# Quantising a convolution's weights beside an involution: where its steps stand in a row, and where the extremes of the first weights are taken

## The chip, the core and the metric

The kernel runs on one core of a Trainium2 chip. The core has TensorE (PE: matrix products, with weight loads shown apart as PEld), VectorE (DVE), ScalarE (ACT), GpSimd (POOL) and SyncE (SP, which here only issues transfers). The engines run side by side and wait for each other through semaphores; each takes its instructions in the order of its own queue. The time is the device time of one execution in microseconds (us), and a kernel's time is the median of its runs.

## The reference

The input is `x`, 8 images of 256 channels and 56 x 56 pixels in float32. Two layers follow each other, each adding its result to its input.

```python
def _L0_conv_ref(x, w_reduce, b_reduce, w_span, b_span):      # an involution, K = 7, G = 16
    ker = einsum('bchw,oc->bohw', x, w_reduce) + b_reduce
    ker = einsum('bchw,oc->bohw', ker, w_span) + b_span       # 49 taps for each pixel and group
    ...
    return (ker * patches).sum(axis=3)                        # over the 7 x 7 neighbourhood

def ternary_quantize(x):
    mx, mn = (jnp.max(x), jnp.min(x))
    lo, hi = mn + (mx - mn) / 3, mx - (mx - mn) / 3
    return jnp.where(x < lo, -1.0, jnp.where(x > hi, 1.0, 0.0))

def noised_tri_conv(x, w):                                    # 3 x 3, 256 to 256 channels
    tq = ternary_quantize(w - jnp.mean(w))
    return conv(x, tq) + einsum('bchw,oc->bohw', x, tq[:, :, 1, 1])

x = x + _L0_conv_ref(_gn(x), ...)                             # _gn: group norm of 32 groups
out1 = relu(batch_norm_train(noised_tri_conv(_gn(x), w1), g1, b1))
out2 = batch_norm_train(noised_tri_conv(out1, w2), g2, b2)
x = x + relu(out1 + out2)
```

The weights `w1` and `w2` (256 x 256 x 3 x 3 each) must therefore be reduced to three numbers each (mean, lower and upper threshold) before any of their elements can be quantised.

## The kernel before

The work has three parts in time. The first is the involution, from the start to about 1170 us. The second is the two convolutions, and the third a last pass over all images that adds `x`, `out1` and `out2`.

**The involution** goes over the 8 images in 4 quarters of 64 channels each, 32 quarters, and over each quarter in 10 rows (`ty`), 320 rows. A row stands for three lines of the image's halves. In a row:

- `apply_row` (PE, L808) multiplies the quarter's matrices `a` with the row's pixels `q` into the PSUM tile `pa`; `transpose_q` (PE L742, ACT L745) makes part of the `q` of later rows, the rest is loaded by `prefetch` (SP, L735) four rows ahead.
- `pick_out` takes `pa` to `inv` (ACT L820, once per row; DVE L821) and adds it to `x` (POOL L824).
- `generate` makes the next quarter's matrices, 14 units per quarter, of which `PER_ROW` gives each row 2, 1 or, in the last row, 0: PE L775 into one of two PSUM tiles `pg`, from which ACT (L779) and DVE (L784) write `a`. A unit's `pg` can be filled again only when they have read the unit two before.
- in between stand the next image's normalisation: statistics (DVE L149), padded strips (`prep`: POOL L667, PE L710, ACT L713, stores from SP at L701), and in an image's third quarter `reduce` (PE L644, ACT L649).

**The order** of each engine's queue is that of the text: `pin()` at a row's end ties each instruction behind the one before it on its engine. Deferred stores stand in the list `tasks`; `transfer(2)` issues up to two of them at the head of a row.

**The weights** are quantised inside these rows by the generator `quantize`, first for `w1`, then for `w2`; from row 8 (`QUANT_AT`) each row runs it to its next `yield`, after `pick_out` and ahead of the row's units of `generate` (L963). For each of the two it takes:

- the extremes, six times: a load of 384 KB (L210), then in the next row a maximum and a minimum (DVE L212, L213) and a sum (ACT L214, in place, hence behind them), then a row with nothing; after the sixth, small operations over five rows make mean and thresholds, with three small PE products (L227, L228, L235). 23 rows.
- 16 pieces of 6 rows: a load of 144 KB (L260); three operations of 288 columns (L263 to L265); two or three of 96 (L275, L279, L280); four of 96 (L282 to L285), after which the store of the seven slots (L288) is put in `tasks`; two rows with nothing. Of the seven stored slots six are used: `SLOT` names them for `weights`.

All pieces share one buffer. The quantised weights are read back from DRAM when the convolutions begin (L301).

**In front of the rows**, the first image is loaded (L545), zeros are stored round the scratch images (L630), the norm's parameters are made, and `reduce(0, py)` for three `py` and the 14 units of quarter 0 run together with the first strips. The tile `a1` that quarter 1's matrices will fill is idle there.

Of the kernel before, what the change touches and what calls it, by code (L numbers as in the profile page):

```python
# [8 lines left out]
F32 = mybir.dt.float32  # L9
F32R = mybir.dt.float32r  # L10
AF = mybir.ActivationFunctionType
ALU = mybir.AluOpType
AX = mybir.AxisListType
# [4 lines left out]
P = 128  # L18
B, C, H, W = 8, 256, 56, 56
HW = H * W  # L20
CT = C // P
# [9 lines left out]
GQ = G // NCQ  # L31
# [4 lines left out]
PY, PX = 3, 8  # L36
TY, TX = 10, W // PX
NP = PY * PX
NT = 2 * (TY - 1) * TX
NE = 2 * TX  # L40
# [15 lines left out]

UNITS = ((0, 3, 0), (3, 3, 0), (6, 2, 0), (8, 4, 2), (12, 4, 1), (16, 4, 2), (20, 4, 1))
NU = GP * len(UNITS)

PER_ROW = (2, 1, 2, 1, 2, 1, 2, 1, 2, 0)  # L60
NQB = 4
# [7 lines left out]
WT = 6  # L69
# [9 lines left out]


QN, QJ = 96, 3 * C // 96
QS = 3 + WT - 2
SLOT = (0, 3, 4, 5, 6, 2)
QM = 6


# [1 line left out]
def involution_tri_block_kernel(  # L88
# [3 lines left out]
    nc = tc.nc  # L92
# [11 lines left out]
    wq_d = [dram.tile([P, QS * CT * 3 * C], F32, tag=f"wqd{i}", name=f"wqd{i}") for i in range(2)]  # L104
# [83 lines left out]
        nc.vector.tensor_tensor(bi, beta, bi, ALU.subtract)  # L188
        return sc, bi

    def quantize(dst, w_dram, pool, transposer, psum_tile, tasks, name):


        nf = CT * 9 * C

        def piece():
            return pool.tile([P, (3 + QS) * QN], F32, tag="piece", name=f"piece_{name}")

        cols = pool.tile([P, 32], F32, tag="cols", name=f"cols_{name}")
        n_cols = [0]  # L200

        def col(n=1):
            n_cols[0] += n
            return cols[:, n_cols[0] - n:n_cols[0]]

        s, mx, mn = col(QM), col(QM), col(QM)
        f = nf // QM
        for j in range(QM):
            v = piece()
            nc.sync.dma_start(v[:, :f], w_dram[:, j * f:(j + 1) * f])  # L210
            yield
            nc.vector.tensor_reduce(mx[:, j:j + 1], v[:, :f], AX.X, ALU.max)  # L212
            nc.vector.tensor_reduce(mn[:, j:j + 1], v[:, :f], AX.X, ALU.min)  # L213
            nc.scalar.activation(v[:, :f], v[:, :f], AF.Identity, accum_out=s[:, j:j + 1])  # L214
            yield
            yield
        sums, ends = col(), col(2)
        nc.vector.tensor_reduce(sums, s, AX.X, ALU.add)
        nc.vector.tensor_reduce(ends[:, 0:1], mx, AX.X, ALU.max)
        nc.vector.tensor_reduce(ends[:, 1:2], mn, AX.X, ALU.min)  # L220
        nc.vector.tensor_scalar(ends[:, 1:2], ends[:, 1:2], -1.0, None, ALU.mult)
        v = piece()
        nc.vector.memset(v[:, :P], 1.0)
        yield

        ps = psum_tile(f"ends_{name}")
        nc.tensor.matmul(ps[:, P:P + 1], v[:, :P], sums, start=True, stop=True)  # L227
        nc.tensor.transpose(ps[:2, :P], ends, transposer)  # L228
        mean, top = col(), col()
        nc.vector.tensor_scalar(mean, ps[:, P:P + 1], 1.0 / (P * nf), None, ALU.mult)  # L230
        nc.vector.tensor_reduce(top[:2], ps[:2, :P], AX.X, ALU.max)
        nc.vector.tensor_copy(v[:2, P:2 * P], top[:2].to_broadcast([2, P]))
        yield
        ps = psum_tile(f"all_{name}")
        nc.tensor.transpose(ps[:, :2], v[:2, P:2 * P], transposer[:2, :2])  # L235
        ex = col(2)
        nc.vector.tensor_copy(ex, ps[:, :2])
        amx, amn = ex[:, 0:1], ex[:, 1:2]

        nc.vector.tensor_tensor(amx, amx, mean, ALU.subtract)  # L240
        nc.vector.tensor_scalar(amn, amn, -1.0, mean, ALU.mult, ALU.subtract)
        yield

        d, q0, r, th = (col() for _ in range(4))
        nc.vector.tensor_tensor(d, amx, amn, ALU.subtract)
        nc.vector.tensor_scalar(q0, d, 1.0 / 3.0, None, ALU.mult)
        nc.vector.scalar_tensor_tensor(r, q0, -2.0, d, ALU.mult, ALU.add)
        nc.vector.tensor_tensor(r, r, q0, ALU.subtract)
        yield
        nc.vector.scalar_tensor_tensor(th, r, 1.0 / 3.0, q0, ALU.mult, ALU.add)  # L250
        nc.vector.tensor_tensor(amn, amn, th, ALU.add)
        nc.vector.tensor_tensor(amx, amx, th, ALU.subtract)
        lo, hi = amn, amx
        yield
        for t in range(CT):
            for j in range(QJ):
                v = piece()
                w, u = v[:, :3 * QN], v[:, 3 * QN:]
                o = (t * QJ + j) * 3 * QN
                nc.sync.dma_start(w, w_dram[:, o:o + 3 * QN])  # L260
                yield
                g = u[:, :3 * QN]
                nc.vector.tensor_scalar(g, w, mean, hi, ALU.subtract, ALU.is_gt)  # L263
                nc.vector.tensor_scalar(w, w, mean, lo, ALU.subtract, ALU.is_lt)
                nc.vector.tensor_tensor(g, g, w, ALU.subtract)  # L265
                yield

                def part(x, k):
                    return x[:, k * QN:(k + 1) * QN]


                c0, c1 = max(C, j * QN) - j * QN, min(2 * C, (j + 1) * QN) - j * QN
                if c0 < c1:
                    g1 = part(u, 1)[:, c0:c1]
                    nc.vector.tensor_scalar(g1, g1, 2.0, None, ALU.mult)  # L275

                e, f = part(w, 0), part(w, 1)
                g0, g1, g2 = (part(u, k) for k in range(3))
                nc.vector.tensor_tensor(e, g0, g2, ALU.add)  # L279
                nc.vector.scalar_tensor_tensor(f, g2, 4.0, g0, ALU.mult, ALU.add)  # L280
                yield
                nc.vector.tensor_tensor(part(u, 3), e, g1, ALU.add)  # L282
                nc.vector.tensor_tensor(part(u, 4), e, g1, ALU.subtract)
                nc.vector.scalar_tensor_tensor(part(u, 5), g1, 2.0, f, ALU.mult, ALU.add)
                nc.vector.scalar_tensor_tensor(part(u, 6), g1, -2.0, f, ALU.mult, ALU.add)  # L285

                def store(u=u, o=t * 3 * C + j * QN):
                    nc.sync.dma_start(  # L288
                        bass.AP(dst[:].tensor, dst[:].offset + o,
                                [[QS * CT * 3 * C, P], [CT * 3 * C, QS], [1, QN]]), u)  # L290

                tasks.append(store)
                for _ in range(3):
                    yield

    def weights(i, k):

# [221 lines left out]
    with ExitStack() as ph1:  # L519
# [16 lines left out]
        fix = ph1.enter_context(tc.tile_pool(name="fix", bufs=1))  # L536
        xpool = ph1.enter_context(tc.tile_pool(name="xpool", bufs=2 * NCQ - 1, side="right"))
        work = ph1.enter_context(tc.tile_pool(name="work", bufs=2))

        def load_x(b, c, j):  # L540

# [68 lines left out]
        ident_sb = fixed([P, P], "ident_sb", ident)  # L610
# [16 lines left out]
        for d in (d for ds in xt_d for d in ds):  # L627
            for r0, n in ((0, PAD), (PAD + HH, HQ - PAD - HH)):
                e = n * QX * RP // P
                nc.sync.dma_start(  # L630
                    bass.AP(d[:].tensor, d[:].offset + r0 * QX * RP, [[e, P], [1, e]]), zero[:, :e])

        def reduce(b, py):

# [242 lines left out]
                gn1_stats(0, c, j)  # L877
        def matrices(m):
            return (apool if m % 2 == 0 else apool1).tile(
                [P, (NT * NP + NE * PX) * GQ], F32, tag=f"a{m % 2}", name=f"a_{m}")  # L880

        apool1 = ph1.enter_context(tc.tile_pool(name="apool1", bufs=1))
        qpool = ph1.enter_context(tc.tile_pool(name="qpool", bufs=NQB))
        pieces = ph1.enter_context(tc.tile_pool(name="pieces", bufs=1))
        pin(start=True)
# [1 line left out]
            pass  # L887
        strips, around = prep(0), surround(0, 0)
        a_next = matrices(0)

        for py in range(PY):
            next(strips)
            transfer(len(tasks))
            reduce(0, py)
        for u, _ in enumerate(generate(0, 0, a_next)):
            if u < 4 or u % 3 == 0 and u < 12:
                next(strips)
                transfer(len(tasks))
            elif u < 9:
                next(around)  # L900
            pin()
            if u == 5:
                for _ in range(NQB):
                    prefetch()
        for _ in around:
            pass


# [8 lines left out]
        for k in rows[:QLEAD]:  # L917
            transpose_q(*k)
        pin()
        norm = iter(())  # L920
        quant = chain(*(quantize(wq_d[i], v, pieces, ident_sb, ps_one, tasks, f"w{i + 1}")
                        for i, v in enumerate((w1, w2))))
        last = None
        for m, (b, c) in enumerate(quarters):
            a = a_next
# [6 lines left out]
            for ty in range(TY):  # L932
# [27 lines left out]
                    gn1_stats(b + 1, (r - 4) // NCB, (r - 4) % NCB)  # L960
                pick_out(b, c, ty, *row)
                next(norm, None)
                if m * TY + ty >= QUANT_AT:  # L963
                    next(quant, None)
                for _ in range(PER_ROW[ty]):
                    next(gen, None)
                if ty % 2 == 0 and m + 1 < len(quarters):
                    next(around)
                pin()
            for _ in gen:  # L970
                pass
# [149 lines left out]
```

## Time and profile before

| what | us |
|---|---|
| median of 3 runs | 2299.33 (2294.78 to 2303.25) |
| the profiled execution's own time | 2293.04 |
| its span, first to last instruction | 2291.3 |
| PE busy / weight loads busy | 1861.3 / 1711.4 |
| DVE busy | 1721.1 |
| ACT busy | 1267.5 |
| POOL busy | 586.5 |
| first start of L820 (row 0) | 64.7 |
| first and last load of a piece of weights (L260) | 190.0 and 936.7 |
| first and last load for the extremes (L210) | 86.7 and 581.9 |
| first read of quantised weights (L301) | 1165.8 |

Busy times are sums over the span and say nothing of which stretch is bound by what; a stretch is read from the busy times inside it and from what ended the waits there. A row of the groups gives the line, the engine, the operation, output and inputs by the program's names, shapes and count, then the busy time, the mean of one in ns, and how long the engine was idle just before them. The granted clock is TensorE's: 1.00 is full speed.

The operations of the quantiser in that execution, mean of one and count:

| line | engine | what | count | ns |
|---|---|---|---|---|
| L212, L213 | DVE | maximum, minimum of 768 columns | 12 each | 945, 941 |
| L214 | ACT | sum of 768 columns, and its read-out | 12 | 843, 187 |
| L263, L264, L265 | DVE | compare, compare, subtract, 288 columns | 32 each | 487, 478, 515 |
| L275 | DVE | doubling of the centre | 16 | 187 |
| L279, L280 | DVE | 96 columns | 32 each | 252, 411 |
| L282, L283, L284, L285 | DVE | 96 columns | 32 each | 273, 328, 464, 255 |

### The profile page before, as it was taken

The numbers are of one execution on the slowest core, as the hardware profiler recorded it, in microseconds if no ns is written. First come the engines' busy times: TensorE is split into PE (matmuls) and PEld (weight loads), VectorE is DVE, ScalarE is ACT, GpSimd is POOL, SyncE is SP. The second block draws the span as 40 slices with busy tenths as digits, with TensorE's granted clock in tenths as the row PEclk, the third lists the DMA queues.
The fourth block names the chain that finished last, engine by engine and source line by source line (L and its number), as shares of the span: only waits on it lengthen the run. The fifth ranks groups of instructions, "written<-read, shape, count | busy, mean of one in ns | idle before, by whom it ended". The sixth has DMA issues, their size and how long they took to land. (4 is left out here: it accounts for less than half of the span.)

```text
span 2291.3 us, 72716 instructions
## 1 busy us (share of the span) xinstructions
PE 1861.3 (81%) x31088; PEld 1711.4 (75%) x31088; DVE 1721.1 (75%) x2906; ACT 1267.5 (55%) x2461; POOL 586.5 (26%) x1320
## 2 busy tenths in 40 slices
PE   5879888887888989999979999999799999980000
PEld 4767777776777777778769999999799999980000
DVE  3666867767578576765679999998899999975444
ACT  2545555454454555555546666665566666673444
POOL 3535545454364554646420000000000000000000
PEclk9989999998999999999999999999899999995555
DMA  4635647565375564745563333333333333369999
GB/s 158 197 105 168 207 138 210 148 183 173 115 216 163 158 208 134 218 136 155 146 240 115 115 115 116 140 141 145 114 140 129 133 115 115 115 240 400 405 431 403
DMA packets 161695, 412.81 MB, mean 180 GB/s; under 512 B 55774, under 2 KB 66396, under 8 KB 154204
## 3 DMA queue, kind: packets, MB, share of 16 engines
q1 hardware_dynamic: 155776, 378.13, 49.1%
q10 hardware_dynamic: 5596, 30.03, 3.2%
q8 instruction: 245, 4.01, 0.7%
q14 instruction: 78, 0.64, 0.1%
HBM read 264.05 MB, written 144.05 MB: 178 GB/s over the span
## 5 line engine op out<-in xcount | busy, mean ns | idle before, releaser
L465 PE MATMUL c<-pl,wq 128*128 128x392 f32 x4608 | 857.3, 348 | 20.2 <-ACT pl L352 20.2
L465 PEld LDWEIGHTS c<-pl,wq 128*128 128x128 f32 x4608 | 855.3, 190 | 22.0 <-ACT pl L352 20.7
L784 DVE TENSOR_TENSOR a<-pg,bt 126x756 f32<-126x756 f32 (+3 forms) x640 | 392.3, 654 | 181.2 <-ACT a L779 125.3
L775 PE MATMUL pg<-kr,wl 64*126 64x140 f32 (+1 forms) x6144 | 456.1, 292 | 60.2 <-DVE a L784 57.3
L775 PEld LDWEIGHTS pg<-kr,wl 64*126 64x126 f32 x6144 | 391.5, 193 | 114.6 <-issue 49.6
L808 PE MATMUL pa<-a,q 126*32 126x48 f32 x17920 | 271.8, 209 | 53.3 <-DVE a L784 28.6
L779 ACT ACTIVATE a<-pg,bt 126x126 f32<-126x126 f32 x768 | 243.6, 476 | 105.4 <-PE pg L775 105.2
L808 PEld LDWEIGHTS pa<-a,q 126*32 126x32 f32 x17920 | 223.1, 112 | 103.0 <-issue 34.2
L824 POOL TENSOR_TENSOR x<-x,inv 128x168 f32<-128x168 f32 x320 | 172.0, 538 | 474.6 <-DVE inv L821 392.8
L821 DVE SCALAR_TENSOR_TENSOR inv<-pa,half_sb,inv 128x168 f32<-128x168 f32 x320 | 116.8, 365 | 176.5 <-ACT inv L820 151.6
L352 ACT CAST pl<-r 128x812 fp32r<-128x812 f32 x192 | 162.5, 868 | 144.8 <-DVE r L347 126.6
L745 ACT COPY q<-ptq 126x384 f32<-126x384 f32 x320 | 138.5, 481 | 161.9 <-issue 91.1
L332 POOL MEMSET xp<- 128x116 f32 x32 | 6.3, 196 | 829.7 <-DVE a L347 829.7
L417 ACT ACTIVATE dummy<-y,nc 128x1568 f32<-128x1568 f32 (+2 forms) x144 | 210.1, 1459 | 5.3 <-DVE y L485 3.5
L353 DVE TENSOR_TENSOR pl<-r,pl 128x812 fp32r<-128x812 f32 x192 | 186.6, 998 | 28.6 <-ACT pl L352 27.4
L667 POOL TENSOR_SCALAR xn<-x,gn 128x224 f32<-128x224 f32 (+2 forms) x384 | 174.0, 473 | 114.6 <-PE pt L710 64.6
L667 POOL TENSOR_SCALAR xe<-x,gn 128x168 f32<-128x168 f32 (+2 forms) x384 | 163.8, 445 | 0.0
L742 PE MATMUL ptq<-ident_sb,xe 128*126 128x128 f32 x960 | 145.5, 288 | 2.5 <-issue 1.2
L149 DVE BATCH_NORM_STATS2 st<-x 128x6 f32<-128x392 f32 x256 | 137.9, 555 | 11.5 <-DMA x<-in_x 9.8
L713 ACT COPY stg<-pt 98x512 f32<-98x512 f32 x128 | 75.3, 588 | 128.5 <-issue 93.0
L820 ACT ACTIVATE inv<-pa,half_sb 128x168 f32<-128x168 f32 x320 | 128.3, 401 | 28.0 <-PE pa L808 25.2
L742 PEld LDWEIGHTS ptq<-ident_sb,xe 128*126 128x126 f32 x960 | 104.8, 143 | 16.8 <-issue 2.2
(144 smaller groups left out, 1828.9 us busy)
## 6 DMA issues: line engine op xcount, KB each, us to landing
q<-xtd SPq DMA_DIRECT2D x320, 252.0 KB
raw<-x1d SPq DMA_DIRECT2D x32, 812.0 KB
raw<-y1d SPq DMA_DIRECT2D x32, 812.0 KB
x<-in_x SPq DMA_DIRECT2D x64, 392.0 KB
xtd<-stg SPq DMA_DIRECT2D x128, 196.0 KB
x1d<-x SPq DMA_DIRECT2D x64, 392.0 KB
y1d<-y SPq DMA_DIRECT2D x30, 784.0 KB
y2d<-y SPq DMA_DIRECT2D x30, 784.0 KB
```

Source lines behind the costliest of these rows:

```text
L352: nc.scalar.copy(hi, r)
L353: nc.vector.tensor_tensor(lo, r, hi.bitcast(F32), ALU.subtract)
L417: nc.scalar.activation(dst, v, f, bias=shift[:, to:to + 1], accum_out=stats[:, to, j, n:n + 1])
L465: nc.tensor.matmul(ps[:, to, :NM], wq[k][:, t, dx, to * P:(to + 1) * P], part[:, t, :, dx:dx + W], start=(c == 0), stop=(c == last))
L667: nc.gpsimd.tensor_scalar(dst[:, i - d - k0:f - d - k0, :, x0:x0 + n], v[:, i:f, :, j0:j0 + n], scale, bias, ALU.mult, ALU.add)
L742: nc.tensor.transpose(pt[:NQ, k * P:(k + 1) * P], xe[c % 2][:, k, PY * ty:PY * ty + QY].rearrange("p r x -> p (r x)"), ident_sb)
L745: nc.scalar.copy(loads[b, c, ty][:NQ, NK:].rearrange("p k c -> p (k c)"), pt[:NQ, :NX * P])
L775: nc.tensor.matmul(dst, wl[rows, c, gp, o:o + NQ], kr[py][rows, px, :], start=True, stop=True)
L779: nc.scalar.activation(whole[:, g0 + i, p0 + j], ps[:NQ, i, j * nt:(j + 1) * nt], AF.Identity, bias=bt[:, c, g0 + i, p0 + j:p0 + j + 1])
L784: nc.vector.tensor_tensor(dst[:, g0:g0 + 2, p0:p0 + nv].rearrange("q g p t -> q g t p"), ps[:NQ, :, t0 * nv:t1 * nv].rearrange("q i (t p) ...
L808: nc.tensor.matmul(ps[o:o + 32, k * 2 * n:(k + 1) * 2 * n], q[:NQ, k, o:o + 32], av[:, t + k, g * 2 * n:(g + 1) * 2 * n], start=True, stop ...
L824: nc.gpsimd.tensor_tensor(xv, xv, iv.rearrange("p t (y x) -> p y t x", x=PX), ALU.add)
```

## The change

- The extremes become a generator of their own, `extremes`. For `w1` all columns are loaded in front in two transfers of 1.18 MB into the idle tile `a1` (made earlier in the text for it), right behind the stores of zeros on SP; two of the six steps run after each of the three `reduce(0, py)`, and the closing arithmetic runs among the units of quarter 0. For `w2` they still go through loaded pieces, between the pieces of `w1` and those of `w2`, with two row ends between a load and its use.
- A row's step of the quantiser stands behind the row's units of `generate` and its `surround`, the last thing before `pin()`.
- A piece takes 7 row ends: load; nothing; L263 and L264; L265, L275 and L279; L280, L282 and L283; L284, L285 and the store's entry in `tasks`; nothing.
- The host lays the three columns of taps out as 1, 0, 2, so that the six stored slots lie together; a piece's tile keeps its size, and a store has 288 KB where it had 336.
- The stores of zeros (L630) are not edited.

```diff
-QS = 3 + WT - 2
-SLOT = (0, 3, 4, 5, 6, 2)
+QS = WT
+SLOT = (0, 2, 3, 4, 5, 1)
...
-    def quantize(dst, w_dram, pool, transposer, psum_tile, tasks, name):
+    def extremes(w, w_dram, cols, pool, transposer, psum_tile, name):
...
         for j in range(QM):
-            v = piece()
-            nc.sync.dma_start(v[:, :f], w_dram[:, j * f:(j + 1) * f])
-            yield
-            nc.vector.tensor_reduce(mx[:, j:j + 1], v[:, :f], AX.X, ALU.max)
-            nc.vector.tensor_reduce(mn[:, j:j + 1], v[:, :f], AX.X, ALU.min)
-            nc.scalar.activation(v[:, :f], v[:, :f], AF.Identity, accum_out=s[:, j:j + 1])
-            yield
+            if w is None:
+                v = piece_of(pool, name)[:, :f]
+                nc.sync.dma_start(v, w_dram[:, j * f:(j + 1) * f])
+                yield
+                yield
+            else:
+                v = w[:, j * f:(j + 1) * f]
+            nc.vector.tensor_reduce(mx[:, j:j + 1], v, AX.X, ALU.max)
+            nc.vector.tensor_reduce(mn[:, j:j + 1], v, AX.X, ALU.min)
+            nc.scalar.activation(v, v, AF.Identity, accum_out=s[:, j:j + 1])
             yield
...
+    def quantize(dst, w_dram, cols, pool, tasks, name):
+        mean, lo, hi = (cols[:, k:k + 1] for k in range(3))
         for t in range(CT):
             for j in range(QJ):
-                v = piece()
+                v = piece_of(pool, name)
...
                 nc.sync.dma_start(w, w_dram[:, o:o + 3 * QN])
                 yield
+                yield
                 g = u[:, :3 * QN]
                 nc.vector.tensor_scalar(g, w, mean, hi, ALU.subtract, ALU.is_gt)
                 nc.vector.tensor_scalar(w, w, mean, lo, ALU.subtract, ALU.is_lt)
+                yield
                 nc.vector.tensor_tensor(g, g, w, ALU.subtract)
-                yield
...
                 nc.vector.tensor_tensor(e, g0, g2, ALU.add)
+                yield
                 nc.vector.scalar_tensor_tensor(f, g2, 4.0, g0, ALU.mult, ALU.add)
-                yield
                 nc.vector.tensor_tensor(part(u, 3), e, g1, ALU.add)
                 nc.vector.tensor_tensor(part(u, 4), e, g1, ALU.subtract)
+                yield
...
-                def store(u=u, o=t * 3 * C + j * QN):
+                def store(u=u[:, QN:], o=t * 3 * C + j * QN):
...
-                for _ in range(3):
-                    yield
+                yield
+                yield
...
+        nf = CT * 9 * C
+        wf = apool1.tile([P, A_COLS], F32, tag="a1", name="wf")
+        for j in range(2):
+            o = j * nf // 2
+            nc.sync.dma_start(wf[:, o:o + nf // 2], w1[:, o:o + nf // 2])
...
+        ext = [extremes(wf[:, :nf], w1, thresholds[0], pieces, ident_sb, ps_one, "w0"),
+               extremes(None, w2, thresholds[1], pieces, ident_sb, ps_one, "w1")]
+        found = ext[0]
...
             reduce(0, py)
+            for _ in range(2):
+                next(found)
         for u, _ in enumerate(generate(0, 0, a_next)):
...
+            next(found, None)
             pin()
...
-        quant = chain(*(quantize(wq_d[i], v, pieces, ident_sb, ps_one, tasks, f"w{i + 1}")
-                        for i, v in enumerate((w1, w2))))
+        made = [quantize(wq_d[i], v, thresholds[i], pieces, tasks, f"w{i + 1}")
+                for i, v in enumerate((w1, w2))]
+        quant = chain(made[0], ext[1], made[1])
...
                 next(norm, None)
-                if m * TY + ty >= QUANT_AT:
-                    next(quant, None)
                 for _ in range(PER_ROW[ty]):
                     next(gen, None)
                 if ty % 2 == 0 and m + 1 < len(quarters):
                     next(around)
+                if m * TY + ty >= QUANT_AT:
+                    next(quant, None)
                 pin()
```

## The prediction

> **What bounds the kernel now.** I read four views: the page's slices, the chain of waits, busy time by stretch, and the instructions in order of time where a stretch is slow.
>
> ```profile
> PE   5879888887888989999979999999799999980000
> DVE  3666867767578576765679999998899999975444
> PEclk9989999998999999999999999999899999995555
> ```
>
> Each digit is one of 40 slices of 57.3 us. The first 20 slices (to 1170 us) are the per-pixel filters; the convolutions follow (to 2057), then the memory-bound last pass. The chain of waits spends 37% on L465 and begins at 1160, at the end of the first part, so it shows nothing the change touches. The edits all lie before 1170; the two convolutions and the last pass issue the same work as before and I carry their 1121 us over. In the first part no engine is full: PE 8 or 9 tenths, DVE 6 to 8. To see what its work on the weights costs I cut it by quarters (10 rows each; L820 runs once per row, so every tenth start of it is a boundary).
>
> ```profile
> 94.70:133.90 39.20, 28.49 (x716) 24.37 (x716) 27.22 (x53) 18.71 (x54) 14.94 (x34) 0.85 0.52 160
> 133.90:187.70 53.80, 44.31 (x921) 38.35 (x923) 27.75 (x73) 22.94 (x61) 17.51 (x40) 0.89 0.29 89
> 249.60:281.30 31.70, 26.05 (x792) 22.45 (x788) 28.09 (x67) 16.61 (x49) 16.10 (x34) 1.00 0.67 189
> 536.80:575.30 38.50, 29.68 (x796) 25.52 (x792) 27.36 (x53) 18.38 (x54) 14.92 (x34) 0.89 0.57 168
> 575.30:624.80 49.50, 42.84 (x924) 36.07 (x926) 27.80 (x76) 22.77 (x61) 17.47 (x40) 0.93 0.32 94
> 967.60:995.60 28.00, 25.75 (x792) 22.23 (x789) 21.77 (x47) 16.27 (x49) 14.96 (x34) 1.00 0.63 184
> 995.60:1038.60 43.00, 40.38 (x918) 34.49 (x919) 21.41 (x54) 21.35 (x56) 17.41 (x40) 0.96 0.34 96
> 1038.60:1067.40 28.80, 27.31 (x806) 23.52 (x804) 17.69 (x35) 17.65 (x50) 18.73 (x43) 1.00 0.61 172
> 1067.40:1096.30 28.90, 27.58 (x808) 23.70 (x806) 17.69 (x35) 17.74 (x51) 18.71 (x43) 1.00 0.59 167
> ```
>
> After the bounds: length, then busy us of PE, weight load, DVE, ACT, POOL, granted clock, DMA share, GB/s. The last piece ends at 948, so the last four lines are quarters **without** weight work: 28.0, 43.0, 28.8 and 28.9 us for the second, third, fourth and first quarter of an image (the third holds next image's reduction), 128.7 per image, with PE 92 to 95% busy. Quarters 0 to 24 last from 64.7 to 967.6, 902.9 us; at these prices they would last 6 x 128.7 + 28.9 = 801. So weight work costs **102 us** now. It splits: extremes of w1, first two lines, (39.2 - 28.0) + (53.8 - 43.0) = **22**. Extremes of w2, rows 127 to 149: quarters 12 (37.3), 13 and 14 exceed by 8.4 + 10.5 + 6.5, less 2 for the pieces in quarter 12's head: **23**. The 32 pieces: the rest, **57**. In the twelve piece quarters that the same view gives a clock of 1.00 the excess is 2.4 us on the mean (0.1 to 5.1); 32 pieces x 6 rows are 19.2 quarters, 46 us; the other 11 come with half clock.
>
> How an extremes step costs so much:
>
> ```profile
> 105.48 2.07 PE L775 MATMUL pg<-kr,wl 64*126 64x126 f32 x16 [2.80 <-DVE a L784]
> ...
> 125.08 0.95 DVE L212 TENSOR_REDUCE cols_w<-piece_w 128x1 f32<-128x768 f32 x1
> 125.95 0.94 DVE L213 TENSOR_REDUCE cols_w<-piece_w 128x1 f32<-128x768 f32 x1
> 126.98 0.84 ACT L214 ACTIVATE piece_w<-piece_w 128x768 f32<-128x768 f32 x1 [2.52 <-DVE cols_w L213]
> 127.82 1.73 ACT L779 ACTIVATE a<-pg,bt 126x126 f32<-126x126 f32 x6
> 129.07 1.53 DVE L784 TENSOR_TENSOR a<-pg,bt 126x504 f32<-126x504 f32 x2 [2.18 <-ACT a L779]
> 130.66 0.62 PE L808 MATMUL pa<-a,q 126*32 126x48 f32 x19 [4.46 <-DVE a L784]
> ```
>
> DVE reduces for 1.9 us; ACT's sum waits for it and holds the row's L779; DVE's L784 waits for that, and PE for L784: 4.46 us. Then PE runs at half clock (granted clock 0.74 over 120 to 140).
>
> **Part 1, w1's extremes go in front.** Removed from the rows: 6 steps and the closing arithmetic, the whole 22 us. Added in front: two loads of 1.18 MB behind the 16 zero stores on SP (issued 12.45 to 23.25), 12 reductions x 0.94 = 11.3 us of DVE, 6 sums x 1.03 (0.84 + 0.19) = 6.2 us of ACT, three small PE products, some 17 small DVE operations of 0.15 to 0.54 us.
>
> ```profile
> 31.71 0.58 ACT L713 COPY stg<-pt 98x512 f32<-98x512 f32 x1
> ...
> 40.00 1.10 DVE L784 TENSOR_TENSOR a<-pg,bt 126x756 f32<-126x756 f32 x2 [15.61 <-PE pg L775]
> ```
>
> DVE is idle for 15.61 us before 40.00: that hides the reductions if the data is there. A load issued at 23.3 lands by 30 and 35 at the 257 GB/s of the first 20 us, by 28 and 31 at the 400 GB/s of the last pass. Taking DVE from 28.5, six pairs end at 39.9 to 40.5. On ACT two sums stand before each L713 (31.71 becomes about 33.7) and partly before the next L649 (0.5 to 0.7 us late). Then DVE's totals wait for the last sum (near 42), so the second and third L784 (41.48, 43.47) come about 1.1 us late, and PE's two closing products wait for DVE between units. I take **+2 us**; bounds 0 (PE is only 15.5 of 20 us busy over 40 to 60) and +8 (late data with ACT holding L649 and L713). The queue behind SP's loads holds the first stage stores, first needed by q loads at 48.69: covered by 14 us.
>
> **Part 2, pieces at the row's end.** The same operations: sum of the rows L263 to L285 over 32 pieces is 113.8 us, 3.56 per piece. Before: three steps of 1.19 us in 3 of 6 rows, between the row's L821 and its first L784. After: four of 0.89 in 4 of 7 rows, behind the row's last L784; the queue behind the step is next row's statistics, L821 and L784. Such a step can use DVE's idle time ahead of next row's L821 and ahead of its first L784; the old place only the latter. In quarter 25 (967.6 on) DVE's idle time, added up from the instructions in order of time, before each row's first L784, from L821 on, is 0, 0, 1.0, 1.0, 0.2, 0, 0, 0, 0.9 and free in row 9, which generates nothing. A 1.19 us step exceeds this by 0.76 on the mean, x 5 steps = 3.8 per quarter; measured 3.7 and 2.4 in the like quarters 5 and 9, so the reckoning is fair. Idle from a row's last L784 to the next first one: 0.1, 1.0, 1.0, 0.2, 0, 0.5, 0, 0.9, 1.7, 2.0. A 0.89 step exceeds it by 0.37, x 5.7 = 2.1. The ratio is 0.55: 2.4 becomes 1.3 per quarter, now over 22.4 quarters: 30 instead of 46. The half-clock part: a piece is now used two row ends after its load, so this wait goes:
>
> ```profile
> DVE piece_w L263 <- DMA piece_w<-in_w: 12.3, 7, 3.3
> ```
>
> and PE's gaps get shorter besides; I leave 4 of 11. Pieces: 57 to 34, **-23**; bounds 0 (the delay only moves into the next row) and -45 (nearly all absorbed). On SP a load now stands behind the row's xa load; a store is issued in the next row, waits for DVE's last step, and holds that row's q load, which is for a row four ahead: about 12 us of cover, and a late row if it were gone. The work ends at row 8 + 32 x 7 + 21 = 253 of 320, before the weights are read at 1165. One slot less stored (336 to 288 KB, 32 times) is DMA off the path: nothing.
>
> **Part 3, w2's extremes at row ends.** Rows 122 to 137, all in quarters 12 and 13. The chain above recurs one row on: 1.9 us DVE, then 1.03 ACT, and behind ACT's sum stand next row's L745, L820 and L779. ACT delay 2.9 us, less the row-end slack of about 0.9: 2.0 x 6 = 12. Does the clock drop too? The Trainium skill (TensorE: Matmul & The Clock Gate, Part 1, "What's actually happening") has the array fall to half clock after an idle window of about 3.4 us. By it, gaps of 2 to 2.9 us would keep full clock: 12 us in all. The row at 105.48 speaks against: after 2.80 us idle, 16 products took 2.07 us, where full clock takes 1.15. By the trace half clock adds a few us; I take 12 + 3 = 15. 23 to 15, **-8**; bounds +5 and -18.
>
> The zeros' stores: no line about them is edited and they keep places 9 to 24 in SP's order, now ahead of the weights' loads. Nothing.
>
> **Sum.** -22 + 2 - 23 - 8 = -51. The profiled execution took 2293.04 (span 2291.3): **2242 us**. It lies 6 us under the runs' median of 2299.33, so a median may come nearer 2248; both are in the range.
>
> **Rivals.**
> (a) Row ends gain nothing, only the front counts: -22 + 2 = -20, 2273. For: idle at row ends is zero in several rows, and PE follows L784 closely. Against: the idle listed above.
> (b) All is hidden: -102 + 2 = -100, 2193. For: over 995.6 to 1038.6 DVE works 21.41 of 43 us. Against: with pieces, DVE in second quarters is already 28.09 of 31.7.
> (c) Slower: each row-end step pushes next row's L821, so pa's buffers and L784 come late by the whole step. 128 steps x 0.89 = 114, + 23 + 2 = 139 against 102: +37, 2330. It decides from (102 - 25) / 128 = 0.60 us lost per step of 0.89. For: L821 stands directly behind. Against: L821 already waits 151.6 us for ACT's L820 in 130 rows.
> (d) Front stall at its bound with no other gain: -22 + 8 and parts 2, 3 at 0 and +5: 2284, no change to speak of.
>
> **Chances.** The forecast, 2213 to 2262: 0.65; (a) 0.18; (b) and what lies near it, under 2213: 0.08; (d) 0.04; (c) 0.05. All parts at their bounds together reach 2208 and 2284; the range 2213 to 2274 holds the forecast and (a). A measurement tells 0.5% (11.5 us) from no change; faster by more 0.91, within 0.04, slower 0.05.
>
> **What would show it.** Quarters 1 and 2 at about 30 and 45 us at clock near 1.00 if part 1 holds; first L820 (64.7) within 5 us; piece quarters near 1.3 us above the lines without weight work; L263's wait on its load gone; quarters 12 and 13 together still some 13 us too long. Wrong if piece quarters stay 2 us long, or if PE's waits on L784 grow.

## The result and the profile after

The changed kernel takes 2265.94 us (median of 4 runs, 2261.97 to 2272.76) beside 2301.29 for the kernel before on the same chip: ratio 0.9854, 95% interval 0.9820 to 0.9888, some 34 us faster. Measured again below it is 0.9833 (0.9809 to 0.9856), 38 us. The forecast was 51 us. The profiled execution takes 2268.19 us (span 2266.3).

The page of the changed kernel, busy tenths in slices of 56.7 us:

```profile
PE   5989898987988989899889999999799999970000
DVE  6757758667576775756689999998999999975444
PEclk9999999998999999999989999999899999995555
```

In the third slice (113 to 170 us) PE is up from 7 to 8 and its clock from 8 to 9; a dip of the clock to 8 stays in the tenth (510 to 567 us), where the extremes of the second weights are. The quarters, cut at the starts of L833 (L820 before), with the same columns as before (length, busy us of PE, weight load, DVE, ACT, POOL, granted clock, DMA share, GB/s):

```profile
93.60:124.50 30.90, 26.54 (x792) 22.68 (x788) 26.49 (x63) 16.50 (x49) 15.37 (x34) 1.00 0.68 185
124.50:170.10 45.60, 42.10 (x918) 36.23 (x919) 23.93 (x67) 21.36 (x57) 17.90 (x40) 0.93 0.37 110
478.00:516.30 38.30, 30.91 (x806) 26.25 (x804) 26.18 (x49) 19.82 (x57) 18.81 (x43) 0.91 0.75 231
516.30:556.60 40.30, 30.08 (x795) 25.54 (x792) 28.43 (x61) 18.40 (x55) 14.88 (x34) 0.90 0.58 165
556.60:603.30 46.70, 42.84 (x920) 37.11 (x921) 24.79 (x73) 21.33 (x57) 18.05 (x40) 0.91 0.34 99
...
1013.50:1041.40 27.90, 27.23 (x808) 23.45 (x806) 17.69 (x35) 17.69 (x51) 18.74 (x43) 1.00 0.62 177
```

Quarters 1 and 2, which held the first weights' extremes, fell from 39.2 and 53.8 us to 30.9 and 45.6, and they now carry pieces. Quarters 12 and 13, which hold the second weights' extremes, did not fall: 38.3 and 40.3, before 37.3 and 38.5 (with quarter 14, into which they reached before, 125.3 in both). Quarter 27, without weights in both, takes 27.9 (before 28.8).

In front, DVE of the changed kernel in order of time:

```profile
29.44 0.95 DVE L215 TENSOR_REDUCE cols<-wf 128x1 f32<-128x768 f32 x1 [4.34 <-DMA wf<-in_w]
...
38.91 0.94 DVE L216 TENSOR_REDUCE cols<-wf 128x1 f32<-128x768 f32 x1
40.24 1.10 DVE L797 TENSOR_TENSOR a<-pg,bt 126x756 f32<-126x756 f32 x2 [0.39 <-PE pg L788]
```

The first half of the weights is there at 29.44, the twelve reductions run without a gap, and the first L797 starts at 40.24 where L784 started at 40.00. The first L833 is at 65.0 (64.7 before): the front costs 0.3 us.

Where did PE's waits go? Before, then after; engine, line and what it waited for, total us, times, longest:

```profile
PE pg L775 <- DVE a L784: 57.3, 58, 3.3
PE pa L808 <- DVE a L784: 28.6, 24, 4.5
PE pa L808 <- issue: 21.5, 24, 2.6
```

```profile
PE pa L821 <- issue: 35.2, 41, 2.6
...
PE pa L821 <- DVE a L797: 19.2, 22, 1.4
...
PE pg L788 <- DVE a L797: 11.7, 16, 2.1
```

The unit's wait for DVE is nearly gone, 57.3 to 11.7 us, of which the extremes of the first weights are a part. The row's products L821 wait 9.4 us less for DVE as well, and stop 13.7 us more under `issue`, where the profile names nothing that they waited for. This is no price of the row's end: the stops lie in the middle of a row's 56 products, none ahead of the first, and with the steps at their old place (below) they add up to 32.0 us too.

### The profile page after: what moved, and what is told of

The parts are those of the page before. It is cut to its first block, busy times and chain, and to the rows that moved or that the text cites. A ratio compares the mean times of both kernels' runs of the same rounds, so it can differ in the third digit from the quotient of the medians.

```text
span 2266.3 us, 72710 instructions
## 1 busy us (share of the span) xinstructions
PE 1864.0 (82%) x31088; PEld 1715.6 (76%) x31088; DVE 1706.3 (75%) x2906; ACT 1267.0 (56%) x2461; POOL 584.2 (26%) x1320
## 4 chain that ended last, share of the span: by engine, by line
PE 57%; DMA 7%; DVE 6%; ACT 3%; issue 2%; POOL 0%; ACTq 0%; DVEq 0%; SPq 0%
PE c L471 37%; PE pg L788 9%; PE pa L821 5%; DMA y1f<-y1d 4%; PE ptq L755 3%; PE pk L657 2%; DVE a L797 2%; DMA out_y<-x1f 2%; DVE x1f L1070 1%; PE pt L723 1%; DMA x1f<-x1d 1%; ACT a L792 1%; DMA y2f<-y2d 1%; ACT dummy L423 1%; DVE y1f L1068 0%
## 5 line engine op out<-in xcount | busy, mean ns | idle before, releaser
L797 DVE TENSOR_TENSOR a<-pg,bt 126x756 f32<-126x756 f32 (+3 forms) x640 | 392.5, 656 | 184.6 <-ACT a L792 147.9
L788 PE MATMUL pg<-kr,wl 64*126 64x140 f32 (+1 forms) x6144 | 453.9, 292 | 19.4 <-DVE a L797 11.7
L821 PE MATMUL pa<-a,q 126*32 126x48 f32 x17920 | 276.2, 209 | 56.4 <-issue 35.2
L821 PEld LDWEIGHTS pa<-a,q 126*32 126x32 f32 x17920 | 225.0, 112 | 110.7 <-issue 51.2
L837 POOL TENSOR_TENSOR x<-x,inv 128x168 f32<-128x168 f32 x320 | 166.3, 520 | 452.2 <-DVE inv L834 384.2
L834 DVE SCALAR_TENSOR_TENSOR inv<-pa,half_sb,inv 128x168 f32<-128x168 f32 x320 | 117.2, 366 | 171.3 <-ACT inv L833 150.9
L758 ACT COPY q<-ptq 126x384 f32<-126x384 f32 x320 | 138.5, 481 | 156.5 <-issue 93.8
L680 POOL TENSOR_SCALAR xn<-x,gn 128x224 f32<-128x224 f32 (+2 forms) x384 | 179.0, 486 | 114.3 <-PE pt L723 62.9
L833 ACT ACTIVATE inv<-pa,half_sb 128x168 f32<-128x168 f32 x320 | 128.3, 401 | 27.2 <-PE pa L821 24.4
```

Of the source, the lines that this page charges most:

```text
L680: nc.gpsimd.tensor_scalar(dst[:, i - d - k0:f - d - k0, :, x0:x0 + n], v[:, i:f, :, j0:j0 + n], scale, bias, ALU.mult, ALU.add)
L758: nc.scalar.copy(loads[b, c, ty][:NQ, NK:].rearrange("p k c -> p (k c)"), pt[:NQ, :NX * P])
L788: nc.tensor.matmul(dst, wl[rows, c, gp, o:o + NQ], kr[py][rows, px, :], start=True, stop=True)
L797: nc.vector.tensor_tensor(dst[:, g0:g0 + 2, p0:p0 + nv].rearrange("q g p t -> q g t p"), ps[:NQ, :, t0 * nv:t1 * nv].rearrange("q i (t p) ...
L821: nc.tensor.matmul(ps[o:o + 32, k * 2 * n:(k + 1) * 2 * n], q[:NQ, k, o:o + 32], av[:, t + k, g * 2 * n:(g + 1) * 2 * n], start=True, stop ...
L837: nc.gpsimd.tensor_tensor(xv, xv, iv.rearrange("p t (y x) -> p y t x", x=PX), ALU.add)
```

## The experiments

Ratios are to the kernel before on the same chip; one thousandth is 2.3 us. Lengths of stretches are from one profiled execution each. Two executions of the changed kernel differ in rows 40 to 120 by 6.6 us (278.7 and 272.1), so a stretch alone decides nothing smaller. Rows 120 to 160 hold the second weights' extremes, but for the front alone (from row 103) and the last experiment (from row 169).

### Front, form and place

The changed kernel once more:

> The changed kernel once more, beside the other kernels of this set and with a trace of its own. Quarters 0 to 25 of the first trace show 25 us gained in the rows (20 of it in rows 8 to 40), the medians 35. Theory F (only the extremes of w1 in front pay, row ends pay nothing): the ratio comes nearer 0.989, about 2275 against 2300. Theory R (row ends pay too, as forecast, and the first trace was an unlucky one in half clock): ratio near 0.982, about 2260.

The changed kernel with the step moved back ahead of the row's units:

```diff
+                if m * TY + ty >= QUANT_AT:
+                    next(quant, None)
                 for _ in range(PER_ROW[ty]):
                     next(gen, None)
...
-                if m * TY + ty >= QUANT_AT:
-                    next(quant, None)
                 pin()
```

> The changed kernel with the row's step put back ahead of the row's units, where it was before; w1's extremes stay in front, the step's 7-row form stays. F: within 4 us of the changed kernel, about 2266 to 2275. R: 20 us or more slower than the changed kernel, about 2287 to 2297, with waits of L788 for L797 back at some 50 us.

The kernel before with the step moved to the row's end, nothing else (the same lines, the other way round):

> The kernel before with nothing but the row's step moved to the row's end; all extremes stay in the rows. F: no change, 2297 to 2305. R: pieces 15 to 23 us and both extremes some 8 us each better, 2262 to 2280.

The old place and the old steps (six rows a piece, one row between a load and its use), with only the first weights' extremes in front (the smaller stores of the changed kernel stay):

> Only the first weights' extremes are moved in front; pieces keep the old six-row form and the old place ahead of the row's units, and the second weights' extremes the old place and one row between load and use. Theory F (the front is worth its whole 22 us and the new piece form next to nothing): 0.9905, about 2274. Theory N (of the old-place kernel's 34 us a good part is the new form, smaller steps and a load two rows ahead): the front alone is also 22, so the difference of 12 us between this kernel and the old-place one is the form. Theory C (the front clears more than its rows' own excess, since less half clock follows): 0.985, as the old-place kernel, 2262.

| kernel | ratio | interval | us less |
|---|---|---|---|
| changed, again | 0.9833 | 0.9809 to 0.9856 | 38 |
| changed, old place | 0.9848 | 0.9823 to 0.9874 | 35 |
| before, new place alone | 0.9945 | 0.9932 to 0.9958 | 13 |
| front alone | 0.9898 | 0.9876 to 0.9921 | 23 |

The front alone is worth 23 us (18 to 28), as reckoned. The new form of the steps adds 11 to it (0.9898 to 0.9848; the intervals only just part). The place alone is worth 13 us with the old steps: neither nothing (F) nor the 20 to 38 of R. That run moves the steps of both weights' extremes too; of the 13.8 us between its profile and the one before, 8.6 lie in the 160 rows of pieces alone (40 to 120 and 160 to 240) and 5.5 in rows 120 to 160. With the new steps the place makes no difference that these totals can tell (0.9848 and 0.9833), as F said.

In the totals, then, form and place do not add up. Why is open. Two opposite effects may hide in it: rows 160 to 240 take 282.1 us at the old place and 276.2 and 272.5 at the row's end, but rows 120 to 160 take 149.5 against 154.7 and 153.2; one profile of the old place is too little to say. A wait that goes is no measure of it either: PE's wait of a unit for DVE is 45.6 us with the front alone, 29.6 with the new steps at the old place and 11.7 at the row's end, and the last of these falls brings no time.

### What the pieces cost, before and after

The changed kernel with the pieces' arithmetic left out; the loads, the stores and the order of rows stay:

```diff
                 yield
                 yield
-                g = u[:, :3 * QN]
-                nc.vector.tensor_scalar(g, w, mean, hi, ALU.subtract, ALU.is_gt)
...
-                nc.vector.scalar_tensor_tensor(part(u, 6), g1, -2.0, f, ALU.mult, ALU.add)
+                nc.gpsimd.memset(u, 0.5)
```

> The changed kernel without the quantising arithmetic of the pieces: each piece is loaded, a constant is written by POOL, and the store goes out, so the quantisation itself is left out and DVE does nothing for the 32 pieces. It prices DVE's 113.8 us of piece work in the rows. As the forecast had it, 30 to 34 us: 2224, 0.969. As the quarters of the changed kernel's profile say, about 50: 2207, 0.961. If the transfers (32 loads of 144 KB and stores of 288 KB) and not DVE were the cost: no more than 10 us faster than the changed kernel.

The same in the kernel before:

> The kernel before, but with the pieces' quantising arithmetic left out (each piece is loaded, POOL writes a constant, the store goes out; steps and place as before). It measures the base of the forecast's second part, which put the pieces at 57 us from the excess of quarters with them over the last, weightless quarters. If the base is right: 0.975, some 2239. If the base was too large (the changed kernel without this arithmetic gained only 17 to 22 us): between 25 and 35 us, 0.985 to 0.989, and the rows 160 to 240 then still stand several us above the weightless price. If the changed kernel merely hides the rest: about 57, since then 35 us of it went with the change.

The changed kernel with no weight work in rows 8 to 302 (`QUANT_AT = 303`, one constant piece, two steps a row):

> The changed kernel with no weight work in rows 8 to 302 (no loads, no stores, no extremes of the second weights, no pieces; constants are stored as weights in the last 17 rows, so quantisation is left out). It is the floor. If the forecast's floor of 128.7 us per image holds in every image, rows 40 to 120 take 257 and rows 160 to 240 take 257. If the earlier images are slower by themselves, they take 262 or more, as they still did without the pieces' arithmetic (264.5 and 268.5), and that part of the 102 us was never the weights'. If the loads and stores are what held those rows, they fall to 257 here: transfers then cost 7 to 11 us per two images.

Ratios: 0.9759 (0.9727 to 0.9792), 0.9859 (0.9832 to 0.9885) and 0.9711 (0.9680 to 0.9743). So the arithmetic costs the kernel before 32 us (26 to 39), not 57, and the changed kernel 17 us against its 0.9833, 22 against its 0.9854. The third total is no clean floor, since its stores run late (from the last row's L810 to the first convolution product 22.4 us, elsewhere 9); its rows are. Rows 40 to 120 and 160 to 240, before:

```profile
218.66:499.49 280.83, 245.63 (x6620) 209.92 (x6618) 201.82 (x487) 146.50 (x402) 148.24 (x320) 0.98 0.60 175
...
654.79:937.09 282.30, 248.82 (x6620) 211.43 (x6618) 199.81 (x483) 147.14 (x402) 143.61 (x320) 0.98 0.60 177
```

The kernel before without the arithmetic:

```profile
221.50:486.03 264.53, 244.22 (x6620) 209.82 (x6618) 163.75 (x358) 146.26 (x401) 147.57 (x333) 0.98 0.63 187
...
638.00:909.98 271.98, 247.81 (x6620) 212.51 (x6618) 164.17 (x358) 146.04 (x401) 147.76 (x333) 0.97 0.63 183
```

No weight work at all:

```profile
191.11:450.91 259.80, 242.62 (x6620) 208.32 (x6618) 163.48 (x358) 145.86 (x401) 139.85 (x320) 0.99 0.56 166
...
579.27:842.96 263.69, 243.78 (x6620) 209.26 (x6618) 163.64 (x358) 145.81 (x401) 139.88 (x320) 0.98 0.56 164
```

These 160 rows hold 26.7 pieces of six rows. DVE's 38.1 and 35.6 us of arithmetic cost 16.3 and 10.3 us, 1.00 us per piece. With it gone the stretches still stand 4.7 and 8.3 us above the kernel with no weights: some 0.5 us per piece stays with the loads, the stores and the constant's writing (single profiles, so a rough figure). And the floor itself is 259.8 and 263.7, not 2 x 128.7 = 257.4. In the changed kernel (22.9 pieces) the arithmetic costs 14.2 and 7.7 us in the first profile, 7.6 and 4.0 in the second, 0.73 us per piece on the mean.

### What the second weights' extremes cost, and why

A unit's 16 products at full clock, and then one of the extremes' steps in the changed kernel, in order of time:

```profile
486.45 1.15 PE L788 MATMUL pg<-kr,wl 64*126 64x126 f32 x16
...
498.73 0.94 DVE L215 TENSOR_REDUCE cols<-piece_w 128x1 f32<-128x768 f32 x1
499.58 0.94 DVE L216 TENSOR_REDUCE cols<-piece_w 128x1 f32<-128x768 f32 x1
...
500.61 0.84 ACT L217 ACTIVATE piece_w<-piece_w 128x768 f32<-128x768 f32 x1 [3.41 <-issue]
501.36 0.19 ACT L217 ACTIVATION_READ_ACCUMULATOR piece_w<-piece_w 128x1 f32 x1
501.45 0.84 ACT L758 COPY q<-ptq 126x384 f32<-126x384 f32 x2
...
502.05 0.61 PE L723 MATMUL pt<-ident_sb,xn 128*98 128x128 f32 x4 [1.08 <-ACT q L758]
502.18 0.41 ACT L833 ACTIVATE inv<-pa,half_sb 128x168 f32<-128x168 f32 x1
...
502.63 0.39 DVE L834 SCALAR_TENSOR_TENSOR inv<-pa,half_sb,inv 128x168 f32<-128x168 f32 x1 [1.16 <-ACT inv L833]
...
502.93 1.50 DVE L797 TENSOR_TENSOR a<-pg,bt 126x504 f32<-126x504 f32 x3
...
503.88 2.07 PE L788 MATMUL pg<-kr,wl 64*126 64x126 f32 x16 [1.21 <-DVE a L797]
```

ACT stands 3.41 us and starts its sum 0.1 us behind DVE's second reduction. (The profile names no releaser here; in another of the six steps, at 488.96, it names L216.) Behind the sum stand the next row's L758 and L833. PE waits 1.08 us for L758. DVE waits 1.16 us for L833, and PE then 1.21 us for DVE's L797, which stands behind that. Its 16 products take 2.07 us where 16 took 1.15: half clock again. The same shows in the waits. Ahead of its six sums ACT stands 19.4 us in the changed kernel, and 6.6 with the sum one row end later (beside the lines shown, 1.0 for L794):

```profile
ACT piece_w L217 <- issue: 16.6, 5, 3.8
ACT piece_w L217 <- DVE cols L216: 2.8, 1, 2.8
...
ACT piece_w L219 <- issue: 2.8, 2, 1.6
ACT piece_w L219 <- DVE cols L216: 2.8, 1, 2.8
```

This experiment leaves DVE's two reductions in one step and gives ACT its sum one row end later:

```diff
             nc.vector.tensor_reduce(mn[:, j:j + 1], v, AX.X, ALU.min)
+            if w is None:
+                yield
             nc.scalar.activation(v, v, AF.Identity, accum_out=s[:, j:j + 1])
```

> The changed kernel with ACT's sum of w2's loaded pieces one row end behind the two reductions, so that ACT no longer stands waiting for DVE (6 rows more). If ACT's wait is what costs (theory S): the extremes of w2, 22 us in quarters 12 and 13 of the first trace, fall to about 12, so 10 us faster than the changed kernel. If it is DVE's 1.9 us in one row (theory D): no change, within 4 us.

And once more, beside other kernels:

> The kernel with the second weights' sum one row end behind its reductions, once more, beside the slots: 0.979 again, within 0.002. If the earlier gain of 11 us over the changed kernel was chance of half-clock stretches, it is nearer 0.983.

0.9787 (0.9767 to 0.9808) and 0.9780 (0.9747 to 0.9812): faster than the changed kernel by 11 us, and than the kernel before by some 50. Rows 120 to 160, changed kernel:

```profile
477.97:632.70 154.73, 131.47 (x3316) 112.48 (x3314) 101.66 (x235) 77.44 (x213) 71.05 (x160) 0.92 0.56 164
```

and with the sum a row later:

```profile
469.01:608.35 139.34, 123.27 (x3316) 104.94 (x3314) 98.77 (x227) 78.17 (x213) 70.82 (x160) 0.99 0.60 179
```

DVE's and ACT's busy times hardly differ; 15 us go, and the clock rises from 0.92 to 0.99. Of the 15, 8.2 are PE's busy time, with as many products (131.5 to 123.3), and 7.2 are its standing (23.3 to 16.1). In the second executions the stretch took 153.2 and 142.7 us. The steps are also spread wider here, six of them over 24 rows and not 18; steps spaced so with the sum left behind its reductions were not run. Two more prices of the same work. Both weights quantised with the first ones' thresholds, the second extremes left out:

> The changed kernel without the second weights' extremes: both weights are quantised with the first ones' mean and thresholds, so a part of the computation is left out. It prices these 23 rows. If they still cost what they did before (22.7 by the quarters of the changed kernel's profile): 2234, 0.973. If, as the forecast had it, 15: 2242, 0.9765.

0.9754 (0.9727 to 0.9780): the second extremes cost the changed kernel 18 us against 0.9833, 23 against 0.9854. The sum a row later gets back about 11 of them. Rows 120 to 160 of the kernel without them:

```profile
470.71:606.05 135.34, 123.87 (x3312) 105.33 (x3310) 95.57 (x235) 73.36 (x202) 72.10 (x160) 0.99 0.60 180
```

So in these profiles the extremes cost the changed kernel 19.4 us there: 11.8 in which PE stands, and 7.6 in which it is busy longer with all but the same products. The second weights' extremes taken in front like the first:

```diff
-        for j in range(2):
+        for i, v in enumerate((w1, w2)):
...
-        quant = chain(made[0], ext[1], made[1])
+        quant = chain(made[0], made[1])
```

> The second weights' extremes are also taken in front, from two more loads of 1.18 MB into the same idle tile and with their six steps among quarter 0's units. Theory S (they cost 20 to 23 us in the rows, because ACT's sum waits for DVE there): rows 120 to 160 fall from 153 to about 133; in front six steps of 1.9 us of DVE and 1.0 of ACT stand among 14 units where PE is not full, cost 5 to 12: 0.977 to 0.980, 2245 to 2250. Theory D (the same DVE work costs as much wherever it stands): 0.983, no difference from the changed kernel.

0.9798 (0.9772 to 0.9823), 9 us faster than the changed kernel by 0.9833, with rows 120 to 160 at 133.0 us. But row 0's L834 is at 80.8, not 65.0, so 16 of some 25 us gained in the rows (beside the changed kernel's second profile) are given back in front, where 5 to 12 had been expected, and for the same reason. ACT there, in order of time:

```profile
50.76 0.84 ACT L217 ACTIVATE wf<-wf 128x768 f32<-128x768 f32 x1 [2.04 <-DVE cols L216]
...
51.61 0.71 ACT L793 ACTIVATE a<-pg,bt 126x126 f32<-126x126 f32 x2
55.04 0.84 ACT L217 ACTIVATE wf<-wf 128x768 f32<-128x768 f32 x1 [2.73 <-DVE cols L216]
```

A sum stands ahead of every unit's L793, and each waits for the reductions behind the last unit's L798. The first weights' six steps had escaped this by running before any unit did.

### Only where DVE is idle

The sum a row later, and the DVE steps only at the ends of six rows of ten (`yield 1` or `yield 2` marks a step that works on DVE; 2 a piece's):

```diff
+        SLOTS, DOUBLE = (1, 2, 5, 7, 8, 9), (8, 9)
+        kind = None
...
-                    next(quant, None)
+                    if kind is None or ty in SLOTS:
+                        was, kind = kind, next(quant, None)
+                        if was == kind == 2 and ty in DOUBLE:
+                            kind = next(quant, None)
```

> The kernel with the second weights' sum a row later, and the pieces' and extremes' DVE steps only at the ends of rows 1, 2, 5, 7, 8 and 9 of a quarter, where DVE was idle between the row's last and the next row's first L784 of a quarter without weights (two steps of a piece may share rows 8 and 9). Same work, last piece about row 270. If what a step costs is what it exceeds that idle time by: a further 5 to 9 us off, 0.975. If idle time at row ends is not what decides: no difference from the kernel with the sum a row later, 0.9785; rows 160 to 240 then stay at 275.

0.9821 (0.9795 to 0.9847): not faster than the sum a row later, by its middle 9 us slower, and in the profiled executions equal (2244.0 and 2243.8 us). That total hides two opposite effects. The rows got faster: row 319's L835 is at 1094.6 us, with the sum a row later at 1122.2. But this order does one piece per quarter and 28 in the rows, not 32 by row 270 as expected, and the other four run behind the rows, where the convolutions begin. SP there, in order of time:

```profile
1111.57 0.33 SPq L266 DMA_DIRECT2D piece_w<-in_w  x1
...
1119.81 0.55 SPq L296 DMA_DIRECT2D wqd<-piece_w  x1
1120.46 0.59 SPq L320 DMA_DIRECT2D raw<-x1d  x1
1122.80 0.33 SPq L266 DMA_DIRECT2D piece_w<-in_w  x1
...
1143.84 0.52 SPq L296 DMA_DIRECT2D wqd<-piece_w  x1
```

and the longest of PE's waits there:

```profile
PE c L473 <- ACT e L483: 26.9, 1, 26.9
```

The four share one buffer and follow each other at 11 to 13 us, with the convolution's loads L320 between them in the same queue. PE stands 26.9 us, to 1148.80: for ACT's L483, whose queue had stood 7.4 us for DVE, whose queue held the last piece to 1143.8. The middle of the convolutions' products is at 1576.2 us in both kernels. In rows 40 to 120, where the slots do 8 pieces, the stretch is 262.75 us, 3.0 above no weight work or 0.37 per piece; with a step in every row it is 272.1 and 269.1, 1.08 and 0.8 per piece of 11.4. Rows 160 to 240, where this order has the second weights' extremes and four pieces begun, take 268.4, 4.7 above no weight work, where the extremes cost the changed kernel 18 to 23. By this one profile the arithmetic costs next to nothing at idle row ends beside the 0.4 to 0.5 that loads and stores leave; with stretches that differ by 6.6 us between executions it is an indication. That all 32 pieces could be placed so within the rows was not run.

## Why the prediction was right and wrong

**Where it landed.** 2265.94 us lies inside the stated range, but in the strip from 2262 to 2274 that was added for rival (a); the second measurement, 2256.84, lies in the forecast's own. The sum was 13 to 17 us too large, and that the range held it is in part owed to its width.

**Right: the direction, and part 1.** Forecast -20 with its +2 in front, measured -23 (18 to 28) for the front alone, which has the smaller stores too. The landing of the loads near 30, the six pairs ending at 39.9 and the hidden cost came as worked out; the front cost 0.3 us, not 2. Quarters 1 and 2 are 30.9 and 45.6 against about 30 and 45. L268 (L263 before) no longer appears among DVE's waits for a load.

**Wrong: part 2, -23.** The failing step is its base: "The 32 pieces: the rest, 57". Taking the arithmetic away from the kernel before gives 32. Of the rest, about 15 (0.5 per piece) stay with loads and stores when the arithmetic is gone, and about 10 were the floor: a single image was taken as the price of six, and quarters 25 to 28 (128.7 us) are cheaper than an image of rows 40 to 240 without weights (130.4 on the mean). The ratio 0.55 was nearer: 17 to 23 of 32 remain, 0.5 to 0.7. With it the part is -9 to -15. The "other 11" of half clock did not fall to 4 either: rows 40 to 120 and 160 to 240 have clocks of 0.98 before and 0.97 after. The forecast's own sign was there: it called itself wrong if piece quarters stay 2 us long, and by its floor the quarters in these rows are 1.8 to 2.7 us long in the changed kernel's two profiles, not 1.3; PE's waits on DVE fell all the same. Two readings were off besides. The 3.56 us per piece add up durations that overlap, where DVE's busy time has 2.8; and the piece quarters at clock 1.00 are fourteen in that view, not twelve, with a mean of 2.5.

**Wrong: part 3, -8.** The mechanism was the one foreseen, ACT's sum behind DVE, one row on; of the term "12 + 3" the 12 came out and the 3 did not. The extremes cost 11.8 us of standing in rows 120 to 160 and 7.6 of longer busy time of PE (11.4 and 6.5 by its second profile), at a clock of 0.92 against 0.99. So half clock was put at 3 and is about 7, and the measured cost is 18 to 23 us, against the 23 reckoned for the kernel before, which no run priced. Quarters 12 and 13 are 22 us too long, not 13. The row of the trace (half clock after 2.80 us of idle) was the right thing to set against the window of about 3.4 us in the Trainium skill (TensorE: Matmul & The Clock Gate, Part 1, "What's actually happening"): at 503.88 half clock is seen again, after stops of 1.08 and 1.21 us, so here the measurement stands against that window. It was then priced at 3 us in all. With the sum a row later the clock and 11 us came back, in two measurements; that the wait itself decides is shown so far as the wider spacing of that run's steps is left aside.

**The rivals.** (a), row ends gain nothing, is the nearest in number (2273), and half right: with the new steps the place itself makes no measurable difference, but the new form does. (c) was not seen: PE waits 1.6 us in all for DVE's L834, the way that it names, and 2.5 before. The pieces' 17 to 23 us are under 0.2 for each of 128 steps, against its deciding 0.60.

With measured sizes the sum is -23, -9 to -15 and 0 to -5: -32 to -43. The two measurements are -34 and -38.

Still open: why the new form is worth as much as the place (its smaller steps and its earlier load were not run apart), and by what way loads and stores cost 0.5 us per piece.

## What to carry to other kernels

Before a cost taken as "stretches with the work less stretches without" is multiplied by anything, split it: work moved to a better place takes only its own share along, not that of its transfers, and not the error of the floor. Where an engine's queue is in order, do not put an instruction that needs another engine's result right behind that result; one row later the extremes cost about half. And when steps are spread thinner, count to the last one: what is left over when the loop ends runs bare.

## What was not expected of the hardware

In the trace's clock records half clock comes in stretches of 3.41 us or multiples of it, and not after long stops alone: at 503.89 us of the changed kernel it begins after stops of PE of 1.08 and 1.21 us. Nor does the same stop always bring it. In row 124 PE stands 2.22 us behind the 29th of 56 products, in both executions of the changed kernel; in the first, 27 products then take 0.85 us, in the second 0.53. The first:

```profile
487.53 0.53 PE L821 MATMUL pa<-a,q 126*32 126x48 f32 x29
...
490.28 0.85 PE L821 MATMUL pa<-a,q 126*32 126x48 f32 x27 [2.22 <-issue]
```

The second:

```profile
485.42 0.53 PE L821 MATMUL pa<-a,q 126*32 126x48 f32 x27 [2.22 <-issue]
```

In rows 120 to 160, with the same instructions, the sum a row later had 3.4 us of half clock in one execution and 13.7 in the other, and the stretch took 139.3 and 142.7 us.

This stop in the middle of a row has no cause that the profile names, and it is not the extremes': PE stands in row 124 for 1.95 us behind the same product with the steps at idle row ends, where the extremes begin at row 169, and for 1.75 us five products earlier with both extremes in front. Many of the stops under `issue` recur so, in both executions of the changed kernel at the same product of the same row. What they are is open.
